# Places, open groups and estimates of a planned four-layer graph kernel: 1024-column places, eight groups, a shorter burst

## The chip, the cores and the metric

The kernel runs on one core of a Trainium2 chip. The metric is the device time of one launch in microseconds (us), the median of several runs. The core has five engines that work beside each other, each through its own queue of instructions in order: TensorE (PE, with its weight loads as PEld), VectorE (DVE), ScalarE (ACT), GpSimd (POOL), and SyncE (SP), which issues the transfers. An engine whose next instruction isn't ready waits, and with it all that stands behind it in its queue.

## The reference

The input x is 128 graphs of 64 nodes with 256 features, fp32, with one 64 x 64 weighted adjacency for all. Four layers follow, each as a residual: x = x + layer(relu(layernorm(x))).

```python
# layer 0: two graph convolutions, then for p = 1..4 an LSTM over windows of p nodes
h = relu(adj @ (x @ Wg0 + bg0));  h = relu(adj @ (h @ Wg1 + bg1))
for p in range(1, 5):
    last = lstm_last(Wih[p-1], Whh[p-1], bih[p-1], bhh[p-1], windows_of(h, p))
    h = h.at[:, every p-th node, :].set(last)
# layer 1: x1 = relu(layernorm(L_norm @ x @ Wc)) + x, with L_norm = 2 L / lambda_max - 1,
#          attention of 4 heads under a mask, @ Wo, layernorm, gelu MLP 256-512-256, layernorm
# layer 2: graph attention, leaky relu of s1_i + s2_j, masked softmax, @ (h W)
# layer 3: h through the eigenvectors U of the normalised Laplacian:
#          U @ (relu((U.T @ h) @ W1 + b1) @ W2 + b2)
```

The largest eigenvalue in layer 1 and the full decomposition in layer 3 depend on the adjacency alone. Everything is fp32.

## The kernel before, in words

**The work.** The 8192 rows are 64 tiles of 128 rows (two graphs to a tile). Layer 0 goes over eight groups of eight tiles (`GT = 8`, `NG = 8`), numbered 0 to 7. Layers 1 to 3 go over sixteen half groups of four tiles (`HT = 4`), numbered 10 to 25 (`REST = 10`). Number 8 loads and prepares the weights of layers 1 to 3 (`WEIGHTS`), number 9 clears four tiles for layer 2, and number 1000 (`EIG`) is the decomposition of a 64 x 64 matrix, a long chain of small VectorE operations that lies beside layer 0.

**The planner.** The kernel's own class `Plan` first records every operation, without issuing it, and then sets one order for all engines in `schedule()`. Each operation has a cost (how long it holds its engine) and a latency, from formulas in `cost()`. The planner keeps a clock for every engine and takes, again and again, the operation that can start first; among those of one engine that can start at once, the one with the lowest `rank()` (L317). The order that comes out is issued by one line (L331), so that all rows of the profile name that line and are told apart by their tiles. The device then runs each queue in that order, at its own pace: the planner's estimates set the order and nothing else.

**Rank.** An operation of an older group comes first. All groups from number `ends` on, which is 10 + 16 - 6 = 20, so the last six, share one rank, and among them the order goes by the length of the remaining path, with a handicap of some microseconds for each group of distance (L322). A transfer's rank is its group.

**Bursts.** Attention in layer 1 multiplies 64 x 64 blocks that lie in the quarters of TensorE's array. Scores and values are each a run of 32 such calls for every half group, recorded between `with plan.burst():` and its end (L103) as one operation with one cost.

**Places.** Values live in pools with numbered places: "bank" (8 PSUM banks), "mid" (512 columns), "stat" (small statistics), "attn", and "big", the one that the change touches. A big value is four tiles of 256 features or two chunks of 512, thus 1024 columns of fp32. Before the change a place of this pool has `HT * (D + 2)`, that is 1032 columns. Eight places are buffers of their own (`NBIG`). `more()` (L934) cuts further ones out of buffers that are done with: the arena (10240 columns, of which the first 4096 are kept for two reloaded groups) when the decomposition is done, `whh[3]` (2048 columns, the recurrent weights of the last LSTM) and the mids (4096) when layer 0 is done, and each of six buffers of x (2048 columns) when its two half groups are done. An operation that needs a place waits, in the plan, until one is free; `reserve()` keeps up to six big places back for the oldest group. A place takes its name in the profile from the buffer that it was cut from, so a big value can show up as `big`, `arena`, `mids`, `Whh` or `x` (and `Wih` holds the weights of layers 1 to 3).

**The window.** `window()` (L945) says how many groups may be under way, counted from the oldest unfinished one: in layer 0 two, and from the last group of layer 0 on, six of the half groups 10 to 25. `slack()` (L953) adds to the time at which an operation counts as ready when the result comes from another engine: 0.4 us for TensorE in layers 1 to 3.

## Time and profile before

| | |
|---|---|
| time, median of 3 runs | 2274.92 us (2273.73 to 2276.86) |
| span of the profiled execution | 2274.8 us |
| TensorE busy | 2244.4 us, 99% |
| weight loads | 1585.8 us, 70% |
| VectorE busy | 1685.7 us, 74% |
| ScalarE busy | 977.3 us, 43% |
| GpSimd busy | 564.0 us, 25% |
| granted clock of TensorE, mean | 0.995 |

Busy is the time in which an engine has at least one instruction running; matmuls overlap, and their ends are modelled, so a row's mean for one matmul is longer than the distance between two. In a group's row, `bank<-big,Wih` reads: written is a PSUM bank, read are a big place and a weight buffer. `[0.97 <-DVE x L331]` says that the engine was idle for 0.97 us before the row and that an operation of VectorE on tile x ended this. A row of the waits has the total, the number of waits and the longest. In time order the run has two stages: layer 0 with the decomposition beside it, up to about 1425 us, and layers 1 to 3 from there.

### The profile page before, as it was taken

How to read it: one execution, taken by the hardware profiler on the slowest of the kernel's cores; microseconds unless marked ns; L12 is line 12 of the kernel's file. 1: busy time of each engine (PE TensorE's matmuls, PEld its weight loads, DVE VectorE, ACT ScalarE, POOL GpSimd, SP SyncE). 2: the span in 40 equal slices, each digit the busy share in tenths (PEclk: the TensorE clock that was granted, in tenths of full speed). 3: DMA queues.
4: the chain of work that ended last, by engine and by line, in shares of the span. 5: the costliest groups of instructions: out<-in, count | busy, mean ns of one | idle time of the engine just before them, and what ended most of it. 6: DMA issues, size and time to landing. Idle time of an engine off the chain costs nothing.

```text
span 2274.8 us, 33569 instructions
## 1 busy us (share of the span) xinstructions
PE 2244.4 (99%) x11316; PEld 1585.8 (70%) x11316; DVE 1685.7 (74%) x6942; ACT 977.3 (43%) x1915; POOL 564.0 (25%) x856
## 2 busy tenths in 40 slices
PE   9999999999999999999999999999999999999997
PEld 6578468468558558558558658767777677776786
DVE  6656666656799999999988823667678868867775
ACT  3333333333323323323433343455555546555763
POOL 3001100200100100100100203454544655555342
PEclk9999999999999999999999999999999999999999
DMA  7000000000000000000000011000000000000001
GB/s 250 0 1 19 1 1 25 32 1 1 1 1 1 1 1 1 1 1 1 5 1 1 7 38 32 1 1 10 11 20 10 10 29 11 29 10 1 2 18 39
DMA packets 27660, 35.48 MB, mean 16 GB/s; under 512 B 3552, under 2 KB 24928, under 8 KB 26976
## 3 DMA queue, kind: packets, MB, share of 16 engines
q1 hardware_dynamic: 26384, 32.29, 4.2%
q8 instruction: 89, 1.46, 0.3%
q10 hardware_dynamic: 1104, 1.05, 0.2%
q14 instruction: 83, 0.68, 0.1%
HBM read 22.85 MB, written 10.49 MB: 15 GB/s over the span
## 4 chain that ended last, share of the span: by engine, by line
PE 91%; DVE 5%; ACT 2%; POOL 1%; issue 1%; DMA 0%; SPq 0%; DVEq 0%; ACTq 0%
PE bank L331 91%; DVE arena L331 1%; DVE stat L331 1%; DVE big L331 1%; DVE x L331 1%; POOL stat L331 1%; ACT arena L331 1%; DVE mids L331 0%; ACT mids L331 0%; ACT big L331 0%; DMA adj<-in_adj_dram 0%; ACT x L331 0%; ACT Wih L331 0%; DVE Whh L331 0%; POOL x L331 0%
## 5 line engine op out<-in xcount | busy, mean ns | idle before, releaser
L331 PE MATMUL bank<-big,Wih 128*128 128x256 f32 (+2 forms) x2592 | 865.1, 476 | 0.9 <-DVE arena L331 0.3
L331 PEld LDWEIGHTS bank<-big,Wih 128*128 128x128 f32 x2592 | 481.6, 190 | 268.4 <-issue 165.9
L331 ACT ACTIVATE mids<-bank,bl 128x256 f32<-128x256 f32 (+2 forms) x624 | 344.2, 562 | 628.6 <-PE bank L331 617.7
L331 PE MATMUL bank<-big,Whh 128*128 128x256 f32 (+3 forms) x1704 | 538.0, 450 | 0.0
L331 PEld LDWEIGHTS bank<-big,Whh 128*128 128x128 f32 x1704 | 319.3, 191 | 140.3 <-issue 74.6
L331 DVE TENSOR_TENSOR arena<-arena 64x21 f32<-64x21 f32 (+6 forms) x2314 | 374.9, 193 | 34.1 <-POOL arena L331 1.0
L331 POOL TENSOR_SCALAR stat<-stat 128x4 f32<-128x4 f32 (+1 forms) x228 | 66.2, 291 | 726.6 <-DVE stat L331 713.0
L331 DVE TENSOR_TENSOR big<-big,mids 128x256 f32<-128x256 f32 (+2 forms) x192 | 93.7, 488 | 163.5 <-ACT mids L331 162.1
L331 DVE TENSOR_TENSOR big<-mids 128x512 f32<-128x512 f32 (+2 forms) x256 | 145.9, 574 | 37.6 <-ACT mids L331 33.7
L331 ACT ACTIVATE mids<-big 128x256 f32<-128x256 f32 (+2 forms) x176 | 89.8, 510 | 103.5 <-DVE big L331 66.8
L331 DVE TENSOR_SCALAR arena<-arena 64x1 f32<-64x1 f32 (+5 forms) x596 | 117.1, 204 | 8.4
L331 POOL TENSOR_TENSOR stat<-stat,mhalf 128x4 f32<-128x4 f32 (+1 forms) x114 | 119.3, 1049 | 6.8
L331 POOL TENSOR_TENSOR arena<-arena 64x1 f32<-64x1 f32 x66 | 41.9, 635 | 311.5 <-DVE arena L331 165.3
L331 PE MATMUL bank<-Wih,big 128*128 128x256 f32 (+1 forms) x520 | 117.6, 362 | 1.2 <-ACT big L331 1.2
L331 PEld LDWEIGHTS bank<-Wih,big 128*128 128x128 f32 x520 | 90.9, 190 | 20.2 <-issue 8.6
L331 ACT COPY big<-bank 128x512 f32<-128x512 f32 x107 | 59.2, 583 | 80.6 <-PE bank L331 65.4
L331 PEld LDWEIGHTS bank<-adjTb,mids 128*128 128x128 f32 x512 | 70.8, 196 | 26.7 <-issue 17.5
L331 ACT ACTIVATE mids<-x,stat 128x256 f32<-128x256 f32 x92 | 48.6, 592 | 89.7 <-POOL stat L331 89.1
L331 DVE SCALAR_TENSOR_TENSOR arena<-arena 64x1 f32<-64x1 f32 (+4 forms) x389 | 77.2, 205 | 10.5 <-POOL arena L331 4.1
L331 POOL MEMSET arena<- 64x2 f32 (+5 forms) x72 | 8.0, 113 | 309.2 <-DVE arena L331 309.1
L331 DVE BATCH_NORM_STATS2 stat<-x 128x6 f32<-128x256 f32 x228 | 83.4, 409 | 0.0
L331 PE MATMUL bank<-adjTb,mids 128*128 128x128 f32 x512 | 73.6, 282 | 3.0 <-ACT mids L331 2.9
(342 smaller groups left out, 3388.6 us busy)
## 6 DMA issues: line engine op xcount, KB each, us to landing
x<-in_x_dram SPq DMA_DIRECT2D x7, 1024.0 KB, 13.7
out_dram<-x SPq DMA_DIRECT2D x24, 256.0 KB, 2.3
Wih<-in_WihT_dram SPq DMA_DIRECT2D x3, 1024.0 KB, 16.6
Whh<-in_WhhT_dram SPq DMA_DIRECT2D x3, 1024.0 KB, 12.3
put<-x SPq DMA_DIRECT2D x2, 1024.0 KB, 4.6
arena<-put SPq DMA_DIRECT2D x2, 1024.0 KB, 5.0
out_dram<-arena SPq DMA_DIRECT2D x8, 256.0 KB, 2.2
Whh<-in_W_dram SPq DMA_DIRECT2D x2, 512.0 KB, 3.7
```

What stands on the lines that cost most here:

```text
L331: getattr(self.engines[op.eng], name)(*map(real, args), **{k: real(a) for k, a in kw.items()})
```

## The change

There are four edits. First, a place of the big pool has `HT * D`, 1024 columns, both for the eight own buffers and where `more()` cuts up the freed ones: the arena then gives 6144 / 1024 = 6 places, `whh[3]` 2, the mids 4, and each x 2. Second, from the last group of layer 0 on, eight groups may be under way. Third, the planner's cost of a burst is 0.1 + 0.034 us a call. Fourth, the handicap among the last six groups is 6 us a group of distance. The aim is to give the planner more ready work for TensorE in layers 1 to 3, and the memory for it, and to bring its clock of TensorE nearer to the device's. The operations recorded are the same ones; what can differ is their order and the places that they use.

```diff
@@ class Plan, burst()
-        self.run.cost = 0.3 + 0.036 * len(self.run.calls)
+        self.run.cost = 0.1 + 0.034 * len(self.run.calls)
@@ class Plan, rank()
-        return (g, 8 * max(op.group - g, 0) - op.path, op.index)
+        return (g, 6 * max(op.group - g, 0) - op.path, op.index)
@@ gnn_kernel
-        "big": [C([P, HT * (D + 2)], f"big{i}") for i in range(NBIG)],
+        "big": [C([P, HT * D], f"big{i}") for i in range(NBIG)],
@@ more()
-        n = HT * (D + 2)
+        n = HT * D
@@ window()
-        return max(oldest, 0) + 2 - oldest if oldest < NG - 1 else max(oldest, REST) + 6 - oldest
+        return max(oldest, 0) + 2 - oldest if oldest < NG - 1 else max(oldest, REST) + 8 - oldest
```

## The prediction

> **What bounds the kernel now.** I read the page's busy shares first, then the busy time by stage, then the waits of TensorE in two of those stages, then the end of TensorE's timeline, and the chain of waits last.

> ```profile
> PE 2244.4 (99%) x11316; PEld 1585.8 (70%) x11316; DVE 1685.7 (74%) x6942; ACT 977.3 (43%) x1915; POOL 564.0 (25%) x856
> ...
> PE 91%; DVE 5%; ACT 2%; POOL 1%; issue 1%; DMA 0%; SPq 0%; DVEq 0%; ACTq 0%
> ```

> TensorE is busy for 2244.4 of 2274.8 us, and the chain that ended last is TensorE's own queue for 91% of it. The change alters no matmul. So the whole question is the 30.4 us in which TensorE has nothing running, and where they lie. By stage (columns: stretch, its length, then the busy time of PE, PEld, DVE, ACT, POOL, then clock and transfers):

> ```profile
> 0.00:1308.00 1308.00, 1301.52 (x5011) 874.66 (x5012) 1029.87 (x5169) 463.85 (x1015) 131.53 (x283) 1.00 0.04 15
> 1308.00:1425.00 117.00, 117.00 (x433) 80.79 (x432) 36.62 (x70) 43.20 (x86) 17.85 (x15) 1.00 0.13 34
> 1425.00:2275.00 850.00, 825.91 (x5875) 630.34 (x5873) 619.19 (x1704) 470.26 (x815) 414.61 (x558) 0.99 0.04 13
> ```

> ```profile
> 2200.00:2275.00 75.00, 60.01 (x358) 53.78 (x356) 45.01 (x140) 27.05 (x52) 23.29 (x38) 0.93 0.11 36
> ```

> Layer 0 with the decomposition beside it (0 to 1425) leaves TensorE idle for 6.5 + 0 us. Layers 1 to 3 (1425 to the end) leave 850 - 825.9 = 24.1 us, of which the last 75 us hold 75 - 60.0 = 15.0. The 775 us from 1425 to 2200 hold only the rest, 9.1. What ends these gaps, first from 1425 to 2200, then from 2200 on:

> ```profile
> PE bank L331 <- DVE x L331: 2.1, 4, 1.0
> PE bank L331 <- ACT mids L331: 2.1, 2, 1.4
> PE bank L331 <- ACT big L331: 2.0, 4, 0.9
> PE bank L331 <- ACT Wih L331: 0.9, 2, 0.6
> PE bank L331 <- DVE mids L331: 0.6, 2, 0.4
> ```

> ```profile
> PE bank L331 <- DVE big L331: 3.8, 1, 3.8
> PE bank L331 <- ACT Wih L331: 2.6, 1, 2.6
> PE bank L331 <- DVE x L331: 2.4, 3, 0.9
> PE bank L331 <- DVE arena L331: 1.0, 1, 1.0
> PE bank L331 <- ACT x L331: 0.7, 1, 0.7
> ```

> The reader is to see fourteen short waits, none over 1.4 us and 7.7 in all, spread over the middle; and in the last 75 us seven waits of 10.5 in all, two of which (3.8 and 2.6) make up 6.4. The last matmul starts nothing that could be hidden: after it comes the last addition and the last write, from 2270.1 to the end, 4.7 us.

> [...] I checked the pace as well, in the timeline of the stage of layers 1 to 3:

> ```profile
> 1853.56 6.17 PE L331 MATMUL bank<-big,Whh 128*128 128x512 f32 x14
> ```

> Fourteen instructions of 512 columns take 6.17 us, 0.44 each, without a gap. TensorE really works at its pace there; little slack hides in "busy". [...] This trace doesn't show a repeating bubble: the gaps are rare and of different lengths. That speaks against a large shortage of places. [...] I cost the other start addresses at nothing. No run here shows that yet. [...] this trace has 49 of them at 1283 ns.

> **The change part by part.**

> *Places of 1024 columns.* No operation gets longer: every large value uses at most 4 x 256 = 1024 columns already. What changes is how many fit. The arena's free part is 10240 - 4096 = 6144 columns: 5 places before, 6 after. Whh3 has 2048: 1, then 2. The mids have 4096: 3, then 4. With the 8 of their own that is 17, then 20 from the start of layers 1 to 3; each finished x of 2048 columns adds 1, then 2, so six of them end at 23, then 32. Before, six groups shared 17 (2.8 each), after, eight share 20 (2.5 each) at first, and more later. It is no large relief early on.

> *Eight groups under way.* TensorE's work in the stage is 825.9 / 16 = 51.6 us a group. The planner always takes the oldest group that is ready, and younger ones fill gaps. With six under way it left 9.1 us of gaps in 775, that is 1.2%. Two more groups give candidates at those points. They can't remove gaps that come from the order's estimates being off, because the engines run the order as written: where TensorE's queue has an instruction whose operand comes 1 us late, everything behind it waits, however much other work exists. Of the 7.7 us of named waits I take half, 3.9. The bounds are 0 (all from estimates) and 9.1 (all from a lack of ready work).

> *The burst's estimate.* A burst of 32 calls was planned at 0.3 + 0.036 x 32 = 1.45 us and is now planned at 0.1 + 0.034 x 32 = 1.19. The timeline shows one:

> ```profile
> 1833.21 1.16 PE L331 MATMUL bank<-big,arena 64*64 64x64 f32 x64
> 1834.30 1.13 PE L331 MATMUL bank<-x,Wih 128*128 128x512 f32 x2
> ```

> The next matmul starts 1.09 us after the burst, so the new estimate is 0.10 off where the old was 0.36 off. Over 32 bursts (2 a group, 16 groups) the planner's TensorE clock loses 32 x 0.26 = 8.4 us. This is no device time; it makes TensorE's planned times agree better with the chip, so that it runs ahead of the others less. I count it inside the half taken above.

> *Weight 6 instead of 8.* It acts on the last six groups alone (`ends`). There each group is preferred by 6 us of remaining path to the next, and no longer by 8, so the six finish closer together and the end has fewer moments with one group alive. In the last 75 us TensorE waits for one group's chain through VectorE: after the matmul at 2237.09 the next starts at 2241.57, 3.78 us of it idle.

> ```profile
> 2237.09 0.70 PE L331 MATMUL bank<-big,same 128*128 128x256 f32 x2
> 2241.57 1.22 PE L331 MATMUL bank<-UTb,big 128*128 128x128 f32 x4 [3.78 <-DVE big L331]
> ```

> I take half of the two large waits as saved, 6.4 / 2 = 3.2, and leave the small ones (4.1), which are the last groups' own chains. Bounds: 10.5 saved at most; on the other side, a smaller distance brings the VectorE-heavy parts of layers 2 and 3 together, and each such collision can cost what this one cost, 3.8.

> *Other engines.* More interleaving can change how often ScalarE swaps tables; ten more would be 12.8 us on an engine busy 470 of 850 us, hidden beside TensorE but for the queue behind it: evacuations to `big`, for which TensorE already waits 2.0 us. Each of the extra groups is opened by four activations into one place; they lie beside layer 0's last group, where TensorE is busy 117 of 117 us. The write back and reload of x moves earlier with its group; transfers fill 4% of the stage. Layer 0's own order keeps its window of 2 until its last group and has no bursts, so all before that group stays.

> Sum: 3.9 + 3.2 = 7.1 us saved, 2274.9 - 7.1 = 2267.8, rounded to 2268.

> **The rivals.**

> *A: the waits only move (30%).* For it: TensorE is at 98.8% from 1425 to 2200, the gaps are short and irregular, and any new order has its own late operands. Against it: the two large waits at the end come where few groups are left. Saving 1 us, it gives 2274.

> *B: slower (13%).* For it: fewer places for each group at the start, 2.5 instead of 2.8, so younger groups hold places that middle ones need; and VectorE, at 619 of 850 us, becomes the wait when the last six bunch. Two more waits of 3.8 at the end, 7.6, less 1.5 saved in the middle: 2274.9 + 6.1 = 2281.

> *C: nearly all gaps close (9%).* For it: the planner may have been held by the six groups alone. Against it: the last group's chain can't be filled. Four fifths of 9.1 + 10.5 = 19.6 are 15.7: 2259.

> **How the numbers follow.** The forecast has 48%, A 30%, B 13%, C 9%. A gain of 0.2% is 4.5 us. Of the forecast 85% passes that, with all of C and 15% of A: 0.41 + 0.09 + 0.04 = 0.54. Slower by 4.5 is nearly all of B and a tenth of A, 0.15. The rest, 0.31, is no change. Closing every gap would end at 2274.9 - 19.6 = 2255.3; the range starts a little above it, at 2257.5, and reaches to 2279.5, into B.

> **What would show it.** Right: TensorE busy for about 2244 us as before, and idle from 1425 to 2200 at about 5 us where it was 9.1; the waits of the last 75 us at about 7 instead of 10.5, with none over 2.5; layer 0 within 1 us. The burst must still take 1.09. Wrong: the same sum of waits under other names (A); a wait of TensorE for VectorE over 3 us more than once in the last 75 us, or waits for places in the middle (B); or a changed pace of matmuls or of vector operations at the new addresses, which no step here contains.

## The result: 17 us faster

The kernel after takes 2258.01 us (median of 4 runs, 2256.42 to 2259.2) against 2275.27 for the kernel before: a ratio of 0.9924, 95% interval 0.9906 to 0.9941. That is 17.3 us less, where 7.1 was forecast. The busy shares on the page of after:

```profile
PE 2236.0 (99%) x11316; PEld 1579.9 (70%) x11316; DVE 1685.2 (75%) x6942; ACT 970.4 (43%) x1913; POOL 561.7 (25%) x856
```

The work is the same, 11316 matmul instructions and 6942 on VectorE. Yet TensorE's busy time fell from 2244.4 to 2236.0 us, which no step of the prediction contained. The profiled span fell by 18.7 (2274.8 to 2256.1), so 8.4 of it is busy time and 10.3 idle time. By stage, with the columns that the prediction gave (stretch, length, busy time of PE, PEld, DVE, ACT and POOL, then clock and transfers):

```profile
0.00:1308.00 1308.00, 1301.39 (x5010) 873.69 (x5011) 1033.19 (x5183) 465.10 (x1017) 134.60 (x291) 1.00 0.05 15
1308.00:1425.00 117.00, 116.26 (x436) 80.26 (x435) 36.75 (x69) 45.92 (x94) 22.23 (x18) 1.00 0.13 34
1425.00:2257.00 832.00, 818.35 (x5874) 625.92 (x5872) 615.29 (x1693) 459.36 (x803) 404.86 (x548) 1.00 0.04 14
```

```profile
1425.00:2181.00 756.00, 752.01 (x5445) 567.16 (x5444) 562.05 (x1535) 427.63 (x743) 376.80 (x506) 1.00 0.03 11
2181.00:2257.00 76.00, 66.34 (x431) 58.76 (x429) 53.25 (x159) 31.73 (x60) 28.06 (x43) 0.98 0.12 42
```

Up to 1425 us TensorE is idle for 7.4 us (6.5 before). From 1425 to 2181 it is 756 - 752.0 = 4.0, where the same part held 9.1. The last 75 us, to the end of the span at 2256.1, hold 75.1 - 66.3 = 8.8, where they held 14.8. And they hold more work: 431 matmul instructions against 358. What TensorE waits for, first from 1425 to 2181, then from there to the end:

```profile
PE bank L331 <- DVE x L331: 1.2, 3, 0.8
PE bank L331 <- ACT big L331: 1.0, 1, 1.0
PE bank L331 <- ACT x L331: 0.7, 1, 0.7
```

```profile
PE bank L331 <- ACT arena L331: 1.1, 2, 0.9
PE bank L331 <- DVE Whh L331: 0.8, 1, 0.8
PE bank L331 <- DVE x L331: 0.8, 1, 0.8
PE bank L331 <- DVE big L331: 0.8, 1, 0.8
PE bank L331 <- DVE mids L331: 0.5, 1, 0.5
PE bank L331 <- DVE stat L331: 0.2, 1, 0.2
```

The five named waits in the middle sum to 2.9 us (fourteen with 7.7 before), those of the end to 4.2 (10.5 before). Both long waits of the end, 3.8 and 2.6, are gone; in layers 1 to 3 no wait is over 1.0. A burst still takes 1.09 us from its start to the next one's (1510.87 to 1511.96 us).

**Where the busy time went.** The granted clock is the column before the last two. Two rows of the kernel before, around its two long waits:

```profile
2220.00:2230.00 10.00, 6.88 (x44) 6.62 (x45) 7.50 (x25) 4.72 (x10) 5.37 (x9) 0.83 0.01 2
...
2240.00:2250.00 10.00, 8.43 (x45) 8.33 (x46) 3.07 (x10) 4.10 (x9) 4.32 (x6) 0.66 0.00 0
```

At each long wait TensorE's clock fell to half for a while: from 2224 to 2227 us and from 2242 to 2247 the column reads 0.50, and outside of the two stretches and their edges 1.00. A mean of 0.83 over 10 us is (1 - 0.83) x 10 / 0.5 = 3.4 us at half speed, and 0.66 is 6.8. So 10.2 us ran at half speed, at most 5.1 us that isn't work; at most, because the second stretch begins within its wait (the column reads 0.90 from 2237.8 to 2241.6, which is 0.8 us). At the start, too, the clock differs between the two profiles (0.91 and 0.94 over the first 57 us), but up to 1425 us TensorE's busy time differs by 0.9 us only (1418.5 and 1417.6). The other 7.6 us of the 8.4 lie in layers 1 to 3. In the kernel after, the column reads 1.00 from 2181 to 2254 us, and the last matmul ends at about 2251.8. The experiments test whether the waits bring it on.

The starts of the matmuls give an estimate of the rest. In these traces the usual distance from one start to the next is 0.11, 0.22 and 0.43 us for instructions of 128, 256 and 512 columns. What the distances in layers 1 to 3 exceed this by, at full clock and without a gap that the profile counts as idle, sums to about 18 us before and 15 after. So some 3 us of the busy time were short waits that the modelled ends of matmuls covered.

### The profile page after: what moved, and what is told of

It reads as the page before. It is cut to its first block, busy times and chain, and to the rows that moved or that the text cites. A ratio compares the mean times of both kernels' runs of the same rounds, so it can differ in the third digit from the quotient of the medians.

```text
span 2256.1 us, 33607 instructions
## 1 busy us (share of the span) xinstructions
PE 2236.0 (99%) x11316; PEld 1579.9 (70%) x11316; DVE 1685.2 (75%) x6942; ACT 970.4 (43%) x1913; POOL 561.7 (25%) x856
## 2 busy tenths in 40 slices
DMA packets 27660, 35.48 MB, mean 16 GB/s; under 512 B 3552, under 2 KB 24928, under 8 KB 26976
## 4 chain that ended last, share of the span: by engine, by line
PE 92%; DVE 5%; ACT 1%; POOL 1%; issue 1%; DMA 0%; SPq 0%; DVEq 0%; ACTq 0%
PE bank L331 92%; DVE arena L331 1%; DVE stat L331 1%; DVE big L331 1%; DVE x L331 1%; DVE mids L331 1%; POOL stat L331 1%; ACT big L331 0%; ACT mids L331 0%; ACT arena L331 0%; DVE Whh L331 0%; POOL x L331 0%; DMA adj<-in_adj_dram 0%; ACT L331 0%; SPq L331 0%
## 5 line engine op out<-in xcount | busy, mean ns | idle before, releaser
L331 PE MATMUL bank<-big,Wih 128*128 128x256 f32 (+2 forms) x2544 | 844.4, 474 | 1.7 <-ACT mids L331 0.6
L331 PEld LDWEIGHTS bank<-big,Wih 128*128 128x128 f32 x2544 | 471.9, 190 | 259.4 <-issue 155.1
L331 ACT ACTIVATE mids<-bank,bl 128x256 f32<-128x256 f32 (+2 forms) x624 | 343.7, 562 | 626.3 <-PE bank L331 616.5
L331 PE MATMUL bank<-big,Whh 128*128 128x256 f32 (+3 forms) x1704 | 513.4, 438 | 0.0
L331 PEld LDWEIGHTS bank<-big,Whh 128*128 128x128 f32 (+1 forms) x1704 | 308.5, 188 | 135.8 <-issue 68.9
L331 DVE TENSOR_TENSOR arena<-arena 64x21 f32<-64x21 f32 (+6 forms) x2316 | 375.4, 193 | 34.6 <-POOL arena L331 1.4
L331 POOL TENSOR_SCALAR stat<-stat 128x4 f32<-128x4 f32 (+1 forms) x228 | 63.6, 280 | 750.4 <-DVE stat L331 737.6
L331 DVE TENSOR_TENSOR big<-big,mids 128x256 f32<-128x256 f32 (+2 forms) x192 | 96.6, 504 | 159.8 <-ACT mids L331 158.4
L331 DVE TENSOR_TENSOR big<-mids 128x512 f32<-128x512 f32 (+2 forms) x256 | 144.4, 569 | 38.4 <-ACT mids L331 35.0
L331 ACT ACTIVATE mids<-big 128x256 f32<-128x256 f32 (+2 forms) x176 | 89.8, 510 | 106.0 <-DVE big L331 69.1
L331 DVE TENSOR_SCALAR arena<-arena 64x1 f32<-64x1 f32 (+5 forms) x596 | 117.1, 204 | 8.4
L331 POOL TENSOR_TENSOR stat<-stat,mhalf 128x4 f32<-128x4 f32 (+1 forms) x114 | 120.5, 1059 | 6.7
L331 POOL TENSOR_TENSOR arena<-arena 64x1 f32<-64x1 f32 x66 | 41.9, 635 | 312.6 <-DVE arena L331 166.4
L331 PEld LDWEIGHTS bank<-adjTb,mids 128*128 128x128 f32 x512 | 69.8, 193 | 27.0 <-issue 17.5
L331 DVE BATCH_NORM_STATS2 stat<-x 128x6 f32<-128x256 f32 x240 | 87.3, 409 | 0.2 <-DMA x<-in_x_dram 0.2
L331 DVE SCALAR_TENSOR_TENSOR arena<-arena 64x1 f32<-64x1 f32 (+4 forms) x389 | 77.3, 205 | 10.5 <-POOL arena L331 4.1
L331 POOL MEMSET arena<- 64x2 f32 (+5 forms) x72 | 8.0, 113 | 309.3 <-DVE arena L331 309.1
L331 PE MATMUL bank<-Wih,big 128*128 128x256 f32 (+1 forms) x376 | 83.4, 358 | 0.0
L331 PE MATMUL bank<-adjTb,mids 128*128 128x128 f32 x512 | 72.6, 279 | 3.3 <-ACT mids L331 2.9
L331 PEld LDWEIGHTS bank<-Wih,big 128*128 128x128 f32 x376 | 64.7, 191 | 9.5 <-issue 2.4
L331 ACT ACTIVATE mids<-x,stat 128x256 f32<-128x256 f32 x72 | 38.1, 591 | 75.5 <-POOL stat L331 74.9
L331 DVE COPY arena<-bank 64x1 f32<-64x1 f32 (+21 forms) x185 | 37.6, 207 | 41.8 <-PE bank L331 31.9
```

Source lines behind the costliest of these rows:

```text
L331: getattr(self.engines[op.eng], name)(*map(real, args), **{k: real(a) for k, a in kw.items()})
```

## The experiments

Theory 1: the edits act in two places. The places, and with them the window, let TensorE's queue find ready work in the middle; the handicap of 6 us ("weight" in the labels) brings the last six groups together and ends the long waits, and with them the halved clock. The burst's estimate does little. Theory 2: any new order gives such a gain. Each difference below is the ratio of its run applied to a time before of 2275 us; so after is at -17.3.

**Undoing one edit at a time.** The four edits are those of the diff above, each taken back alone.

*Places of 1032 columns again*

```diff
-        "big": [C([P, HT * D], f"big{i}") for i in range(NBIG)],
+        "big": [C([P, HT * (D + 2)], f"big{i}") for i in range(NBIG)],
...
-        n = HT * D
+        n = HT * (D + 2)
```

> The kernel after with the places of 1032 columns again (17 instead of 20 at the start of layers 1 to 3), all else as after. Theory 1, the places are what eight open groups live on: with eight groups on 17 places the young ones hold places that the middle ones need, and TensorE's queue runs dry early in layers 1 to 3. By the planner's own clock it is idle there for about 40 us more than in the kernel after; so about 2290 us (2280 to 2300), slower than before too. Theory 2, any new order gives some such gain, and the places are no shortage (the forecast counted 2.8 places a group before and 2.5 after and called it no large relief): within 5 us of the kernel after, 2253 to 2263.

Measured 2300.22 us, ratio 1.0107 (1.0093 to 1.0120): 24 us slower than before and 42 slower than after, a hair above theory 1's range. TensorE's named waits in layers 1 to 3 sum to 38.5 us, where after has 7.1. From 1500 to 1550 us the clock is 0.76 on average, by the sum above 24 us at half speed, so at most 12 us more. Theory 2 falls.

*Six groups again*

```diff
-    ... max(oldest, REST) + 8 - oldest
+    ... max(oldest, REST) + 6 - oldest
```

> The kernel after with six groups under way again, all else as after. Theory 1, the places do most of the work and the window little: the middle of layers 1 to 3 stays at about the unused time of after, 2261 us (2257 to 2264). Rival, the two further groups are what fills TensorE's gaps: the 9 us that the middle gained come back, 2267 us.

Measured 2262.68, ratio 0.9943 (0.9930 to 0.9955), -13.0: some 4 us of the gain go, as theory 1 has it, though this interval and that of after just overlap. The named waits from 1425 to 2187 sum to 5.4 us, where after has 2.9.

*The old estimate of a burst*

```diff
-        self.run.cost = 0.1 + 0.034 * len(self.run.calls)
+        self.run.cost = 0.3 + 0.036 * len(self.run.calls)
```

> The kernel after with the old estimate of a burst, 0.3 + 0.036 a call. Theory 1, the estimate is within the noise of the others: 2258 us, within 2. Rival, the truer clock of TensorE is what removed the short waits in the middle: 2262 to 2267 us, with named waits from 1425 to 2200 back at 7 to 8 us.

Measured 2260.89, ratio 0.9933 (0.9921 to 0.9946), -15.2. It is 2 us from after, at the edge of what theory 1 gave, and the intervals overlap. The named waits from 1425 to 2183 sum to 4.8 us, between the 2.9 of after and the 7.7 of before. The rival's larger loss isn't seen.

*The handicap of 8 us again*

```diff
-        return (g, 6 * max(op.group - g, 0) - op.path, op.index)
+        return (g, 8 * max(op.group - g, 0) - op.path, op.index)
```

> The kernel after with the handicap of 8 us a group again among the last six. Theory 1, the end of the run gains from this edit alone: the last 76 us take 9 us longer, TensorE's clock is halved there again for 5 to 10 us after waits of over 2 us, 2267 us. Theory 2, the end is as good with any order that the places and the window give: 2258 to 2260 us and no halved clock.

Measured 2268.57, ratio 0.9968 (0.9956 to 0.9980), -7.3: 10 us of the gain go. TensorE's timeline at its end:

```profile
2213.87 0.66 PE L331 MATMUL bank<-ident,Wih 128*128 128x128 f32 x4 [2.58 <-ACT Wih L331]
2215.20 2.05 PE L331 MATMUL bank<-big,x 128*128 128x128 f32 x16 [0.68 <-ACT big L331]
...
2231.98 1.22 PE L331 MATMUL bank<-UTb,big 128*128 128x128 f32 x4 [3.78 <-DVE big L331]
2233.00 1.06 PE L331 MATMUL bank<-ident,Wih 128*128 128x128 f32 x4
```

The two waits of the kernel before are back to the hundredth, 2.58 and 3.78. After the first, the clock stays whole here (sixteen instructions in 2.05 us), after the second it doesn't (four take 1.06, as they do in the kernel before, where the column reads 0.50). This trace is of the fastest of the six runs: its mean clock is 0.998, that of the slowest two 0.995, and they took 2270.4 and 2270.7 us. That suggests that whether a wait of 2.6 us is followed by a halved clock can differ between runs of one and the same order. Theory 1's size is right, and the time at half speed is within what it gave: the clock of the last 76 us is 0.95, by the sum above some 7.6 us.

**One edit alone on the kernel before.**

*The handicap of 6 us alone.*

> The kernel before with the handicap of 6 us a group among the last six, nothing else. Theory 1, the end gains from this edit, about as much as it lost where it was undone (9 us): 2266 us, the last 76 us with no halved clock of TensorE, everything up to 2000 us as before. Theory 2, the end is good only with what the other edits leave to it: within 3 us of before.

Measured 2266.4, ratio 0.9960 (0.9947 to 0.9972), -9.1. The last 76 us, of the kernel before, then of the handicap of 6 alone:

```profile
2198.80:2274.80 76.00, 61.21 (x363) 54.69 (x361) 46.21 (x145) 28.23 (x54) 23.29 (x38) 0.93 0.11 35
```

```profile
2188.40:2264.40 76.00, 67.43 (x437) 60.02 (x436) 55.56 (x163) 32.76 (x62) 29.49 (x44) 0.99 0.12 42
```

With 6, the end holds 437 matmul instructions instead of 363 in the same time, and 55.6 us of VectorE's work instead of 46.2. The clock reads 0.99 over these 76 us, where the kernel before has 0.93. The bunching does bring VectorE's work together, as rival B feared, but TensorE has more to do meanwhile. The edit is worth 9 to 10 us in either company.

*The places alone, six groups.*

> The kernel before with places of 1024 columns, six groups under way as before, nothing else. Theory 1, six groups hold fewer places than the 17 they had, so more of them bring little by themselves: 2273 to 2276 us. Rival, the shortage of places was the cause of the short waits in the middle: 2266 us.

Measured 2281.19, ratio 1.0026 (1.0017 to 1.0035): 5.9 us slower than before. Both expectations missed. The new order has one long wait in the middle, and the clock is halved with it (0.77 from 1615 to 1630, 6.9 us at half speed). The two long waits of the end are as before (2.59 and 3.79), and the sixteen instructions of 128 columns behind the first take 3.78 us (3.67 in the kernel before). Of TensorE's timeline, the wait in the middle:

```profile
1623.46 1.22 PE L331 MATMUL bank<-mids,same 128*128 128x256 f32 x2 [4.78 <-DVE mids L331]
```

*The burst's estimate alone.*

> The kernel before with the new estimate of a burst, nothing else. Theory 1, the estimate only redraws the order; by the planner's own clock TensorE then is idle for 10 us more than in the order of before, 2285 us (2279 to 2289). Rival, a truer estimate makes every order better: 2268 to 2273 us, the named waits in the middle halved.

Measured 2298.23, ratio 1.0101 (1.0085 to 1.0116): 23 us slower, twice what theory 1 gave. Its waits in the middle are several of 3 to 4 us; one, and then the clock in three short stretches around such waits (busy PE, PEld, DVE, ACT, POOL, then the clock):

```profile
1840.41 1.13 PE L331 MATMUL bank<-big,same 128*128 128x256 f32 x2 [3.59 <-DVE big L331]
```

```profile
1525.00:1545.00 20.00, 14.33 (x64) 10.98 (x63) 9.64 (x33) 9.66 (x16) 3.60 (x6) 0.83 0.00 0
1830.00:1845.00 15.00, 10.08 (x52) 7.37 (x51) 12.84 (x31) 9.99 (x18) 8.68 (x8) 0.89 0.01 1
1885.00:1896.00 11.00, 6.17 (x29) 5.17 (x30) 10.06 (x36) 7.98 (x14) 7.16 (x14) 0.69 0.00 1
```

Half-speed time is (0.17 x 20 + 0.11 x 15 + 0.31 x 11) / 0.5 = 17 us, so at most 8.5 us on top of the waits. The named waits from 1425 to 2220 sum to 23.6 us, some 16 more than the 7.7 of before to 2200. So the plan, which had 10 us more of idle time, missed about 6 us of waits, and the halved clock can account for the rest of the miss. That it does is an estimate; no run here fills these waits. An estimate nearer to the device made a worse order.

**Is it the count of places, or their size and addresses?** The kernel after, with places of 1024 columns but only as many as before:

```diff
-        for i in range(ap.shape[1] // n):
+        for i in range(ap.shape[1] // (n + 8)):
```

> The kernel after, places of 1024 columns at the new addresses, but only as many of them as before (17 instead of 20 at the start of layers 1 to 3). Theory, the count of places is what eight open groups need: as with 1032 columns, 2300 us, with the long wait at about 1510 to 1525 us. Rival, the new size and start addresses make the operations themselves quicker, or the order was unlucky: 2258 to 2265 us.

Measured 2300.44, ratio 1.0110 (1.0096 to 1.0123), the same as with 1032 columns. TensorE's timeline shows the wait at the named place:

```profile
1524.19 1.22 PE L331 MATMUL bank<-big,same 128*128 128x256 f32 x2 [16.61 <-DVE big L331]
```

While TensorE waits these 16.6 us, VectorE, ScalarE and GpSimd carry one chain of small operations on big places, and what comes next in TensorE's queue needs its result. That the other groups had nothing to offer because the places were taken is the theory's reading; the trace doesn't name the groups. So it is the count and not the size, for this order: the run with 1032 columns has the same waits (16.61 and 3.16 us), so the two are one order that the planner made of 17 places, and 18 or 19 places weren't run. The start addresses, which the prediction costed at nothing as its author's estimate, do cost nothing that can be measured (2300.44 us against 2300.22).

**Do the waits halve the clock?** The kernel before, with matmuls that nobody reads put into TensorE's queue ahead of its two long waits (`fill` names the two positions in the order):

```diff
-            for op in order:
+            for n, op in enumerate(order):
+                if n in self.fill:
+                    k, b, w, o = self.fill[n]
+                    for _ in range(k):
+                        self.engines["PE"].matmul(self.pools["bank"][b], o, w, start=True, stop=True)
...
```

> The kernel before with six extra matmuls of 128x512 that nobody reads, in TensorE's queue just ahead of the two long waits of the end: two ahead of the wait of 2.6 us, four ahead of that of 3.8 us, so that TensorE computes while it waits. Theory, the long waits cost twice, once as waits and once because TensorE's clock is halved for 10 us after them: with the waits filled the clock stays whole and the end is shorter by about half of 10 us, 2270 us, though work was added. Rival, the halved clock has nothing to do with the waits, or costs nothing since the end hangs on other engines: 2275 us or a little more.

Measured 2272.62, ratio 0.9987 (0.9980 to 0.9993), -3.0, with six matmuls added. The same sixteen instructions behind the first long wait, in the kernel before and then with the wait filled:

```profile
2222.44 0.66 PE L331 MATMUL bank<-ident,Wih 128*128 128x128 f32 x4 [2.59 <-ACT Wih L331]
2223.77 3.67 PE L331 MATMUL bank<-x,x 128*128 128x128 f32 x16 [0.68 <-ACT x L331]
```

```profile
2216.39 1.88 PE L333 MATMUL bank<-Wg,ones 128*128 128x512 f32 x4
2219.14 0.66 PE L335 MATMUL bank<-ident,Wih 128*128 128x128 f32 x4 [0.87 <-ACT Wih L335]
2220.47 2.05 PE L335 MATMUL bank<-x,x 128*128 128x128 f32 x16 [0.68 <-ACT x L335]
```

They take 2.05 us instead of 3.67, and the four of `ident,Wih` behind the second wait 0.60 instead of 1.06. So in this order the waits do bring on the halved clock, and that has a price, about 3 us of the 5 expected.

The mean clocks on record say the same without an added matmul. Of the 31 runs of the kernel before that were measured beside this one, nine had a mean clock of 0.995 and took 2276.9 us on average, and four had 0.998 and took 2273.1. All 21 runs with the waits filled had 0.997 or more. The halved clock is thus partly a matter of chance from run to run, and it is worth about 4 us. The handicap of 6 us alone took 2266.5 us in its four runs at 0.998, 6.6 less than the kernel before at that clock, which is about the 6.4 us of the two long waits; the rest of its 9.1 would be the clock. The kernel after took 2258.4 us in its three runs at 0.998. By this estimate, whose mean clocks have the start of the run in them too, about 15 of its 17 us would have come at an equal clock, and 2 to 3 came by the clock.

**The two edits that need each other, and two other orders.** First the places and the window alone on the kernel before.

> The kernel before with the two edits that need each other, places of 1024 columns and eight groups under way, and neither of the two others. Theory, the four edits work as one order of which the planner's own clock tells the idle time, and that is 8.6 us less than before: 2266 us (2263 to 2270), the end still with its long waits and halved clock. Rival, the parts add up: this is what is left of the gain after the end's 9 us and the burst's, about 2269 to 2275.

Measured 2272.98, ratio 0.9985 (0.9977 to 0.9994), -3.4. The rival's range held, the theory's did not. In the middle (to 2195 us) the named waits are down to 6.1 us, and the end is as before, with its 3.78 and 2.59. Then two settings whose order, by the planner's own clock, is better than that of after:

```diff
-        self.run.cost = 0.1 + 0.034 * len(self.run.calls)
+        self.run.cost = 0.2 + 0.034 * len(self.run.calls)
-        return (g, 6 * max(op.group - g, 0) - op.path, op.index)
+        return (g, 5 * max(op.group - g, 0) - op.path, op.index)
-    ... max(oldest, REST) + 8 - oldest
+    ... max(oldest, REST) + 7 - oldest
```

> The kernel after with seven groups, a burst at 0.2 + 0.034 a call, and a handicap of 5 us: an order in which TensorE, by the planner's own clock, is idle for 3.7 us less in layers 1 to 3 than in the kernel after. Theory, that clock tells a few us: 2254 us (2252 to 2257). Rival, below some 5 us it tells nothing and the order is a draw: 2258 to 2265.

Measured 2259.15, ratio 0.9928 (0.9915 to 0.9940).

```diff
-        self.run.cost = 0.1 + 0.034 * len(self.run.calls)
+        self.run.cost = 0.15 + 0.034 * len(self.run.calls)
-        return (g, 6 * max(op.group - g, 0) - op.path, op.index)
+        return (g, 5 * max(op.group - g, 0) - op.path, op.index)
```

> The kernel after with a burst at 0.15 + 0.034 a call and a handicap of 5 us, eight groups as in the kernel after: idle for 3.6 us less than in the kernel after by the planner's own clock. Theory, that clock tells a few us: 2254 us (2252 to 2257). Rival, below some 5 us it tells nothing and the order is a draw: 2258 to 2265.

Measured 2262.11, ratio 0.9940 (0.9926 to 0.9954). Neither beats the kernel after; the rival holds. In both, three waits close together come with a halved clock again, though none is long by itself; of the first one's timeline and then its stretch of 10 us (clock 0.83, so 3.4 us at half speed; in the second the twelve instructions behind the third wait take 2.90 us, in the first 2.48, where 0.11 each would be 1.3):

```profile
2195.25 0.71 PE L331 MATMUL bank<-Ub,arena 128*128 128x128 f32 x4 [1.02 <-ACT arena L331]
2196.67 0.66 PE L331 MATMUL bank<-ident,Wih 128*128 128x128 f32 x4 [0.70 <-ACT Wih L331]
2198.86 2.48 PE L331 MATMUL bank<-Ub,arena 128*128 128x128 f32 x12 [1.54 <-ACT arena L331]
```

```profile
2195.00:2205.00 10.00, 7.51 (x46) 6.97 (x47) 9.71 (x25) 6.71 (x14) 3.68 (x4) 0.83 0.01 2
```

So the idle time in the plan tells large differences apart, though not their size: its 40 us were 42 and its 10 were 23, its gain of 8.6 was 3.4 (the places and the window), and its gains of 3.7 and 3.6 were none. In the table, "weight" is the handicap of 6 us and "burst" the new estimate.

| kernel | us against before |
|---|---|
| weight alone | -9.1 |
| places alone | +5.9 |
| burst alone | +23.0 |
| places and window | -3.4 |
| places, window, burst | -7.3 |
| places, window, weight | -15.2 |
| places, burst, weight | -13.0 |
| window, burst, weight | +24.3 |
| all four | -17.3 |

## Why the prediction was right, and where its sizes were off

The direction and the stage held, and so did both mechanisms, as far as single orders show: the gain lies in layers 1 to 3, from waits that became fewer in the middle and at the end, and layer 0 stayed within 1 us. The size did not. The gain was 2.4 times the forecast, the likeliest time 10 us too high, and the time lies in the range by 0.5 us (2258.0, where the range begins at 2257.5); that it does is owed to the width of the range. What came is nearly rival C, "nearly all gaps close", which had 9%. One of the prediction's own signs failed: TensorE's busy time did not stay at 2244. Of the 18.7 us between the two profiles, 11.1 are idle time of layers 1 to 3 and 7.6 their busy time. The terms of the sum:

- *The end, 3.2 us: mis-sized.* It measured 9.1 alone and 10.0 with the other three edits. The step took half of the two long waits. Both went wholly (6.4), and they had a second cost that the step lacked, the halved clock that came with them, about 3. The prediction showed the clock column of that very row, 0.93 in the last 75 us, and passed over it. For this reason its floor was wrong as well: "closing every gap" was worked out with 2244.4 us of busy time as fixed, and 8.4 of that went.
- *The middle, 3.9 us: mis-sized.* Idle time there fell by 5.1, and the three edits without the weight measure 7.3. Some of the short waits lay under the modelled ends of matmuls and so within busy time, which the sum took as work; the estimate above gives about 3 us of this.
- *"No large relief early on", of the places: wrong.* I divided places by groups, 2.8 and 2.5, and took the average for the need. With 17 places for eight groups the kernel is 42 us slower than with 20: its named waits are 31 us longer, one of them 16.6, and the clock is 0.76 from 1500 to 1550 us, around that one. The mean doesn't say who holds the places. Alone, at six groups, they cost 5.9: the forecast had two independent edits where there is one. The rare, short gaps of before, which I took as a sign against a shortage by estimate alone, came from six groups and couldn't show what eight would need.
- *The burst inside the half: right in effect, wrong in reason.* With the places and the window it is worth 2 to 4 us (-3.4 to -7.3, and -15.2 to -17.3, both about the width of the intervals). Alone it costs 23. "TensorE's planned times agree better with the chip" is no gain by itself.
- *Addresses, transfers, table loads at nothing: right.* The count, not the address, mattered; the bytes moved are the same (35.48 MB), and ScalarE loads its tables 47 times instead of 49, at 1283 ns each.
- *Rival B: its mechanism did occur* (VectorE's work bunched at the end, 46.2 to 55.6 us in 76), and was hidden beside TensorE.

What stays open: why the truer estimate alone makes so bad an order, and which instructions hold the places in the stall. Each setting gives one order, so that effects of 2 to 6 us, of the window and the estimate above all, may be those of one lucky or unlucky order; only a series of orders for each setting would tell. The window alone on 1032-column places wasn't run; the case without the places, +24.3, stands near it.

## What to carry to other kernels

A wait of the engine that bounds the kernel can cost more than its length (here 2.59 and 3.78 us of waits came with 10.2 us at half the clock): look at the granted clock in short stretches behind each long wait, and behind short ones that lie close together (three of 1.02, 0.70 and 1.54 us came with 3.4 us of it), before taking busy time as work. Count half of the half-speed time as the most that removing the wait may bring on top; here 3 to 4 us of 5 came. Compare the mean clock of several runs, too (0.995 to 0.998 for the kernel before), since one profile shows one chance. In a kernel whose order is planned, settings that share a resource, here groups under way and places, are one edit: the places alone cost 5.9 us, eight groups without the places ended 24 us above the kernel before, and the two together gained 3.4. And an estimate of cost is worth what the order that comes out is worth; try it on the device in the company in which it will stay.
